# Row maxima of 384 and 512 keys taken by one fused VectorE instruction that adds the causal mask

## The chip, the cores and the metric

The kernel runs on one core of a Trainium2 chip. The metric is the device time of one execution in microseconds. The kernel before has a median of 1715.19 us over 3 runs (1712.28 to 1717.48).

## What is computed

The reference chains four layers over an input of 4 batches of 1024 tokens with 128 channels: a time-mixing layer with an exponential scan, a mixture of 16 small experts with grouped routing, a linear attention with decaying state ("deltanet"), and a causal softmax attention with grouped keys, followed by a mixture of 8 experts. The change concerns the causal softmax attention alone:

```python
def _gqa(x, wq, wk, wv, wo):
    q = (x @ wq.T).reshape(B, S, N_HEADS, HEAD_DIM)      # 16 heads of 8
    k = (x @ wk.T).reshape(B, S, N_KV_HEADS, HEAD_DIM)   # 4 key heads
    v = (x @ wv.T).reshape(B, S, N_KV_HEADS, HEAD_DIM)
    k = jnp.repeat(k, n_rep, axis=2)
    v = jnp.repeat(v, n_rep, axis=2)
    attn = jnp.einsum('bqhd,bkhd->bhqk', q, k) * scale
    causal = jnp.tril(jnp.ones((S, S), dtype=bool))
    attn = jnp.where(causal, attn, jnp.float32(-jnp.inf))
    attn = jax.nn.softmax(attn, axis=-1)
    out = jnp.einsum('bhqk,bkhd->bqhd', attn, v).reshape(B, S, C)
    return out @ wo.T
```

Here S is 1024 and B is 4. A softmax needs the largest score of each row. The kernel computes these row maxima in a pass of its own, ahead of the exponentials.

## The kernel before

Up to about 711 us of the span the first three layers run, in an order that a planner chooses from the program. From there on the order is written out by hand (`tc.manual_schedule()`): the causal attention of the four batches is worked in 32 blocks, one for each batch b and each i of 0 to 7, a block being 128 query rows of all 16 heads. Between the units of a block the same loop feeds in, one step per tick, the remaining linear attention of later batches and the building of queries and keys (`front`), and the last expert layer of earlier rows (`behind_it`). [...]

For block (b, i) the row maxima are computed by `maxima(b, i)`, two blocks before the block's weights (`AHEAD = 2`), and its units are interleaved with the units of `weighted`. A unit of `weighted` multiplies keys by queries (L945), takes the exponential on ScalarE (L950), masks the diagonal on GpSimd (L954), and later adds the product with the values (L937).

`maxima` splits the keys of a row into the half that holds the diagonal (`late`) and, for i of 4 and more, a full first half of 512 keys (`early`). The number of keys in the diagonal half is n_s = 128, 256, 384 or 512, by i % 4. [...] `late` puts 4, 2, 1 or 1 heads into one bank (`in_bank`). It issues one score matmul for each head (L874), then one matmul that adds the causal mask to the last 128 keys of each head in the bank (L878: the identity times `later`, a bf16 tile that holds 0 or -1e30), and then one maximum over the bank on VectorE (L882). `early` has no mask: a matmul (L886) and a maximum (L887). All of them share three PSUM banks (`to_max`, the tile name `sm`): a fourth matmul group waits until VectorE has read the first bank.

When the 16 heads are done, `rows` combines the two halves (L894), splits each maximum into three bf16 parts (L895 to L898), and, some ticks later, transposes them (L901), copies them out of PSUM (L905) and stores them by DMA into rows of the query tile (L909). The score matmul at L945 then subtracts the maximum as part of its product.

For i % 4 of 2 or 3 (384 or 512 keys) there is one head in a bank, so a block has 16 units of one score matmul, one mask matmul and one maximum. There are 16 such blocks in the four batches, so 256 such units. These are what the change touches. Other VectorE work that stands in the same queue: the state scans of the linear attention (L620), its products with the queries (L637), and the small operations of the last expert layer.

Of the kernel before, what the change touches and what calls it, by code (L numbers as in the profile page):

```python
# [12 lines left out]
BF = mybir.dt.bfloat16  # L13
AF = mybir.ActivationFunctionType
ALU = mybir.AluOpType
# [3 lines left out]
P = 128  # L19
NB = 4  # L20
T = 1024
CH = 512
# [12 lines left out]
def r3(ap, a):  # L35
    return ap.rearrange("p (a b) -> p a b", a=a)
# [3 lines left out]
def sandwich(ctx: ExitStack, tc: tile.TileContext, x, vecs, cmats, rope, wa, wb, wc, wd, out):  # L40
# [3 lines left out]
    nc = tc.nc  # L44
# [121 lines left out]
    def restarts(nb, n_e, pool, name):  # L166

        t = pool.tile([P, nb, n_e], FP, name=name, bufs=1)
        nc.gpsimd.memset(t, 1.0)
        nc.gpsimd.memset(t[:, :, 0:1], 0.0)  # L170
        return t
# [580 lines left out]
    pk = ctx.enter_context(tc.tile_pool(name="pk", bufs=1, side="left", reuse_waits="tile"))  # L752
# [8 lines left out]
    m = pe.tile([P, P], FP, tag="a", name="m", bufs=1)  # L761
    make_causal_mask(nc, m, MASKED)
    for k in range(4):
        nc.gpsimd.tensor_copy(later[:, k, :], m)
    wv_d, wo_d, wgate_d = wdt[:, 160:192], wdt[:, 192:320], wdt[:, 320:328]
    restart8 = restarts(4, 8, pk, "restart8")
    QSCALE = float(1.0 / np.sqrt(8).astype(np.float32))
# [22 lines left out]
    def later_on(ticks, fn):  # L790
        due.append((now[0] + ticks, fn))
# [67 lines left out]
    def maxima(b, i):  # L859


        qr, kr = qrs[b, i // 4], keys_r[b % 2]
        tb = slice(i % 4 * P, (i % 4 + 1) * P)
        half = i // 4
        n_s = (i % 4 + 1) * P
        in_bank = CH // n_s
        ms = pe.tile([P, 2, 16], FP, tag="ms", name="ms", bufs=3)

        def late(h0):
            sc = to_max([P, CH], "sm")  # L870
            view = r3(sc[:, : in_bank * n_s], in_bank)
            for k in range(in_bank):
                h = h0 + k
                nc.tensor.matmul(  # L874
                    view[:, k, :], lhsT=qr[0:KROWS, h, tb], rhs=kr[0:KROWS, half, h // 4, 0:n_s],
                    start=(k == 0), stop=False, skip_group_check=True,
                )
            nc.tensor.matmul(  # L878
                view[:, :, n_s - P :], lhsT=identb, rhs=later[:, :in_bank, :], start=False, stop=True,
                skip_group_check=True,  # L880
            )
            nc.vector.tensor_reduce(ms[:, 0, h0 : h0 + in_bank], view, AX.X, ALU.max)  # L882

        def early(h):
            sc = to_max([P, CH], "sm")
            nc.tensor.matmul(sc, lhsT=qr[0:KROWS, h, tb], rhs=kr[0:KROWS, 0, h // 4, :], start=True, stop=True)  # L886
            nc.vector.tensor_reduce(ms[:, 1, h : h + 1], sc, AX.X, ALU.max)  # L887

        def rows():
            mp = pe.tile([P, 3, 16], BF, tag="mp", name="mp", bufs=3)  # L890
            left = pe.tile([P, 16], FP, tag="ml", name="ml", bufs=3)
            top = ms[:, 0]
            if half:
                nc.vector.tensor_max(top, top, ms[:, 1])  # L894
            nc.vector.tensor_copy(mp[:, 0], top)  # L895
            nc.vector.tensor_sub(left, top, mp[:, 0])
            nc.vector.tensor_copy(mp[:, 1], left)
            nc.vector.tensor_sub(mp[:, 2], left, mp[:, 1])  # L898
            def turned():
                pm = to_max([48, P], "m_ps", BF)  # L900
                nc.tensor.transpose(pm, mp.rearrange("p i h -> p (i h)"), identb)  # L901

                def kept():
                    mt = pe.tile([48, P], BF, tag="mt", name="mt", bufs=3)
                    nc.vector.tensor_copy(mt, pm)  # L905

                    def placed():
                        for k in range(3):
                            nc.sync.dma_start(  # L909
                                out=qr[KROWS + k : KROWS + k + 1, :, tb], in_=mt[16 * k : 16 * k + 16, :]  # L910
                            )
                        placed_rows.add((b, i))

                    later_on(3, placed)

                later_on(1, kept)

            later_on(9, turned)

        units = [lambda h0=h0: late(h0) for h0 in range(0, 16, in_bank)]  # L920
        if half:
            units += [lambda h=h: early(h) for h in range(16)]
        return units + [rows]
# [243 lines left out]
    pd = ctx.enter_context(tc.tile_pool(name="pd", bufs=2, side="right", reuse_waits="tile"))  # L1167
# [111 lines left out]
```

## Time and profile before

| | |
|---|---|
| median of 3 runs | 1715.19 us |
| profiled execution | 1715.55 us |
| its span | 1713.8 us |
| TensorE busy | 1310.6 us, 76% |
| VectorE busy | 1168.9 us, 68% |
| ScalarE busy | 856.7 us, 50% |
| GpSimd busy | 655.9 us, 38% |
| DMA | 90.49 MB, mean 53 GB/s |
| mean granted TensorE clock | 0.85 |
| from 711 us to the end: TensorE, VectorE busy | 803.6 us, 672.3 us of 1002.8 |

The page gives, for one profiled execution on the chip, the busy time of each engine, the span in 40 slices, the chain of work that ended last, and the costliest groups of instructions. A group's row names the source line, the engine, the operation, output and input tiles with their shapes and the count; then its busy time and the mean duration of one; then the idle time of the engine just before it and what ended that idle time. PE is TensorE's matmuls, PEld its weight loads, DVE is VectorE, ACT ScalarE, POOL GpSimd, SP SyncE. [...] the busy time of a group can be more than the time the queue loses to it: two instructions of one engine can overlap in part. A wait names the waiting instruction and the one that released it, with the total, the count and the longest.

### The profile page before, as it was taken

Reading aid. Unit: us, or ns where it says so; the run is one execution under the profiler, and the core shown is the slowest. Engines: PE = TensorE matmul, PEld = TensorE weight load, DVE = VectorE, ACT = ScalarE, POOL = GpSimd, SP = SyncE. Lnnn points to the kernel's source line nnn. Section 1 sums busy time; section 2 is a strip of 40 time slices with the busy share of each in tenths; the row PEclk is TensorE's granted clock in tenths of the full one; section 3 lists DMA queues with packets and bytes.
Section 4 is the critical chain, followed back from the end, with each engine's and each line's share of the span. In section 5 each row is a group of like instructions: output and inputs, shape, how many; then the busy total and the mean of one; then the engine's idle time right before and its main releaser. Section 6 shows DMA issues by size and latency. Waiting matters only on the chain.

```text
span 1713.8 us, 15167 instructions
## 1 busy us (share of the span) xinstructions
PE 1310.6 (76%) x4593; PEld 463.3 (27%) x4604; DVE 1168.9 (68%) x1991; ACT 856.7 (50%) x1565; POOL 655.9 (38%) x663
## 2 busy tenths in 40 slices
PE   2547887867865889678779869888887879889864
PEld 1213333312221323133223223322232223233311
DVE  4575676698775877867995597777779825577601
ACT  3457776624453457234436625645553345645561
POOL 5554353524252324323433363427227333122212
PEclk8669998978887999877779869987898669989996
DMA  2000110313033122101112111231113011110101
GB/s 97 13 7 6 25 50 25 96 40 108 13 111 110 53 65 85 44 12 34 45 58 70 53 57 54 70 92 46 38 37 101 21 48 64 45 61 29 54 22 56
DMA packets 59330, 90.49 MB, mean 53 GB/s; under 512 B 9904, under 2 KB 26800, under 8 KB 58544
## 3 DMA queue, kind: packets, MB, share of 16 engines
q1 hardware_dynamic: 59248, 89.52, 17.3%
q8 instruction: 36, 0.59, 0.1%
q14 instruction: 46, 0.38, 0.1%
HBM read 76.38 MB, written 12.71 MB: 52 GB/s over the span
## 4 chain that ended last, share of the span: by engine, by line
PE 32%; DVE 18%; ACT 6%; issue 4%; POOL 4%; DMA 2%; SPq 0%; POOLq 0%; DVEq 0%; ACTq 0%
PE av L937 8%; PE sc L945 5%; DVE ms L882 4%; DVE st L620 4%; ACT pr L950 3%; PE sm L874 3%; DVE ms L887 3%; PE y L1074 3%; PE sm L886 2%; PE ln_v L138 2%; PE num_ps L674 1%; POOL hid L473 1%; POOL share L1062 1%; PE sm L878 1%; PE g_ps L138 1%
## 5 line engine op out<-in xcount | busy, mean ns | idle before, releaser
L950 ACT ACTIVATE pr<-sc 128x512 f32<-128x512 f32 x576 | 328.2, 595 | 361.7 <-PE sc L945 358.0
L882 DVE TENSOR_REDUCE ms<-sm 128x1 f32<-128x512 f32 (+3 forms) x352 | 210.5, 633 | 114.2 <-PE sm L878 103.0
L945 PE MATMUL sc<-qr,keys_r 75*128 75x512 bf16 x576 | 234.1, 422 | 37.7 <-ACT pr L950 28.7
L887 DVE TENSOR_REDUCE ms<-sm 128x1 f32<-128x512 f32 x256 | 165.0, 682 | 56.4 <-PE sm L886 55.9
L937 PE MATMUL av<-pr,va 128*32 128x512 f32 x1152 | 183.1, 710 | 0.0
L954 POOL TENSOR_SCALAR_AFFINE_SELECT pr<-pr 128x512 f32<-128x512 f32 x128 | 89.4, 712 | 244.5 <-ACT pr L950 236.2
L874 PE MATMUL sm<-keys_r,qr 72*128 72x512 bf16 (+3 forms) x512 | 138.2, 337 | 46.3 <-DVE ms L882 43.9
L138 PE MATMUL ln_v<-rs,cm 128*128 128x512 f32 x176 | 113.0, 733 | 43.0 <-ACT rs L126 28.3
L473 POOL TENSOR_TENSOR hid<-hid,gate 128x512 f32<-128x512 f32 x64 | 81.9, 1280 | 162.9 <-DVE hid L468 124.6
L614 POOL TENSOR_TENSOR kv<-vrep,phi 128x512 f32<-128x512 f32 x64 | 85.6, 1342 | 115.0 <-issue 47.9
L1062 POOL TENSOR_TENSOR share<-n,every 128x512 f32<-128x512 f32 x64 | 87.2, 1373 | 91.1 <-DMA every<-row 70.5
L455 PE MATMUL y_ps<-hid,wbt 128*128 128x512 f32 x144 | 84.1, 669 | 46.3 <-DVE hid L474 44.4
L886 PE MATMUL sm<-keys_r,qr 72*128 72x512 bf16 x256 | 99.6, 417 | 25.0 <-DVE ms L887 20.6
L945 PEld LDWEIGHTS <-keys_r 75*128 75x128 bf16 x576 | 58.7, 106 | 153.2 <-issue 126.3
L878 PE MATMUL sm<-later,identb 128*128 128x128 bf16 (+2 forms) x341 | 90.5, 265 | 0.0
L474 DVE TENSOR_TENSOR hid<-hid,g 128x512 f32<-128x512 f32 x72 | 57.7, 801 | 46.7 <-POOL hid L473 39.9
L138 PE MATMUL u_ps<-n,wbt 128*128 128x512 f32 x144 | 77.3, 618 | 7.6 <-DVE hid L468 5.1
L138 PE MATMUL g_ps<-n,wbt 128*128 128x512 f32 x144 | 78.8, 630 | 3.7 <-DVE hid L463 1.6
L1074 PE MATMUL y<-share,wexp 128*128 128x512 f32 x128 | 70.8, 644 | 9.6 <-POOL share L1062 9.4
L874 PEld LDWEIGHTS <-qr 72*128 72x128 bf16 x512 | 51.0, 107 | 99.4 <-issue 82.8
L465 ACT ACTIVATE g<-hid 128x512 f32<-128x512 f32 x72 | 45.1, 626 | 55.4 <-DVE hid L463 55.3
L674 PE MATMUL num_ps<-st,cm 128*32 128x512 f32 x128 | 52.5, 777 | 25.7 <-DVE st L637 25.5
(300 smaller groups left out, 2394.9 us busy)
## 6 DMA issues: line engine op xcount, KB each, us to landing
gate<-rows SPq DMA_DIRECT2D x64, 256.0 KB
vrep<-v_rows SPq DMA_DIRECT2D x64, 256.0 KB
every<-row SPq DMA_DIRECT2D x64, 256.0 KB
qr<-dq SPq DMA_DIRECT2D x72, 128.0 KB
turn<-in_rope_dram SPq DMA_DIRECT2D x8, 512.0 KB
dq<-qp SPq DMA_DIRECT2D x8, 384.0 KB
keys_r<-dk SPq DMA_DIRECT2D x72, 32.0 KB
sums<-av_sb SPq DMA_DIRECT2D x128, 18.0 KB
```

What stands on the lines that cost most here:

```text
L138: nc.tensor.matmul(ps, lhsT=lhsT, rhs=rhs, start=True, stop=True)
L473: nc.gpsimd.tensor_mul(a, a, gate)
L874: nc.tensor.matmul(view[:, k, :], lhsT=qr[0:KROWS, h, tb], rhs=kr[0:KROWS, half, h // 4, 0:n_s], start=(k == 0), stop=False, skip_group_ch ...
L878: nc.tensor.matmul(view[:, :, n_s - P :], lhsT=identb, rhs=later[:, :in_bank, :], start=False, stop=True, skip_group_check=True,)
L882: nc.vector.tensor_reduce(ms[:, 0, h0 : h0 + in_bank], view, AX.X, ALU.max)
L886: nc.tensor.matmul(sc, lhsT=qr[0:KROWS, h, tb], rhs=kr[0:KROWS, 0, h // 4, :], start=True, stop=True)
L887: nc.vector.tensor_reduce(ms[:, 1, h : h + 1], sc, AX.X, ALU.max)
L937: nc.tensor.matmul(pavs[b, i][32 * g : 32 * g + 32, :], lhsT=va[:, j, g, :], rhs=pr, start=(j == 0), stop=(j == i),)
L945: nc.tensor.matmul(sc, lhsT=kr[0:ROWS, j // 4, g, j % 4 * P : (j % 4 + 1) * P], rhs=qr[0:ROWS, 4 * g : 4 * g + 4, tb], start=True, stop=True,)
L950: nc.scalar.activation(pr, sc, AF.Exp)
L1062: nc.gpsimd.tensor_mul(shares[-1], n4, gates[len(shares) - 1])
L1074: nc.tensor.matmul(y, lhsT=wexp[:, e, :], rhs=shares[e], start=False, stop=(e == 7))
```

## The change

For 384 and 512 keys the mask matmul is left out, and the plain maximum is replaced by one instruction that adds a mask from SBUF and takes the maximum of the sum:

```diff
+    at_last = pk.tile([P, CH], BF, name="at_last")
+    nc.gpsimd.memset(at_last, 0.0)
+    nc.gpsimd.tensor_copy(at_last[:, CH - P :], m)
...
                 nc.tensor.matmul(
                     view[:, k, :], lhsT=qr[0:KROWS, h, tb], rhs=kr[0:KROWS, half, h // 4, 0:n_s],
-                    start=(k == 0), stop=False, skip_group_check=True,
+                    start=(k == 0), stop=(in_bank == 1), skip_group_check=True,
                 )
+            if in_bank == 1:
+
+                masked = pd.tile([P, CH], BF, tag="masked", name="masked", bufs=1)
+                nc.vector.tensor_tensor_reduce(
+                    masked[:, :n_s], sc[:, :n_s], at_last[:, CH - n_s :], 1.0, -3.0e38, ALU.add, ALU.max,
+                    ms[:, 0, h0 : h0 + 1],
+                )
+                return
             nc.tensor.matmul(
                 view[:, :, n_s - P :], lhsT=identb, rhs=later[:, :in_bank, :], start=False, stop=True,
                 skip_group_check=True,
```

`at_last` is a constant of 512 columns per partition in bf16: zero in the first 384, the causal mask in the last 128. The slice `at_last[:, CH - n_s :]` has the mask in its last 128 columns for either size. The instruction reads the scores from PSUM and the mask from SBUF, writes the masked scores as bf16 to `masked`, a buffer that nothing reads, and writes the maximum to `ms`. Blocks with 128 and 256 keys, and the unmasked first halves, keep their code. In the changed kernel the lines stand further down: the score matmul is L877, the fused instruction L884, the remaining mask matmul L889, the remaining plain maximum L893, the maximum of the first half L898.

## The prediction

> **What bounds the kernel now.** I read the chain of waits on the page first, then the groups by shape, the waits, and the timeline and stage sums where the changed line runs.
>
> ```profile
> PE 32%; DVE 18%; ACT 6%; issue 4%; POOL 4%; DMA 2%; SPq 0%; POOLq 0%; DVEq 0%; ACTq 0%
> PE av L937 8%; PE sc L945 5%; DVE ms L882 4%; DVE st L620 4%; ACT pr L950 3%; PE sm L874 3%; DVE ms L887 3%; PE y L1074 3%; PE sm L886 2%; PE ln_v L138 2%; PE num_ps L674 1%; POOL hid L473 1%; POOL share L1062 1%; PE sm L878 1%; PE g_ps L138 1%
> ```
>
> No engine sets the end alone: TensorE leads, VectorE is second, and the row maxima (L882, 4%) stand among the dearest links. The mask matmul (L878) is 1%.
>
> ```profile
> L882 DVE TENSOR_REDUCE ms<-sm 128x1 f32<-128x512 f32 x128 | 82.3, 683 | 28.3 <-PE sm L878 28.3
> L882 DVE TENSOR_REDUCE ms<-sm 128x1 f32<-128x384 f32 x128 | 64.7, 546 | 21.2 <-PE sm L878 21.0
> L878 PE MATMUL sm<-later,identb 128*128 128x128 bf16 x256 | 62.5, 244 | 0.0
> L468 DVE TENSOR_TENSOR hid<-u_ps,hid 128x512 f32<-128x512 f32 x72 | 49.1, 682 | 15.0 <-PE u_ps L138 10.1 <-ACT g L465 3.9 <-ACT ho L699 0.7
> L620 DVE TENSOR_TENSOR_SCAN st<-beta_ps,kv 128x512 f32<-128x512 f32 x32 | 38.0, 1209 | 7.6 <-POOL kv L614 7.6
> ```
>
> The first three rows are exactly what changes: 256 maxima and their 256 mask matmuls. The last two are the nearest rows to the new instruction.
>
> ```profile
> DVE ms L882 <- PE sm L878: 103.0, 73, 7.1
> PE sm L874 <- DVE ms L882: 43.9, 44, 4.4
> ```
>
> Both engines wait on each other around the three PSUM buffers of `to_max`: VectorE for the last matmul of a bank, TensorE for a bank to be read. The 103 us are not the price of the mask matmul. With it gone, VectorE waits for the score matmul just before it.
>
> The 256 units come in 16 stretches of 16 (blocks with i % 4 of 2 or 3, four batches). Each stretch runs from the first to the last of its reductions; four of the 16, and their sum:
>
> ```profile
> 1008.35:1026.93 18.58, 14.15 (x68) 5.08 (x69) 18.53 (x26) 6.17 (x11) 10.88 (x9) 0.68 0.12 34
> ...
> 1392.24:1418.98 26.74, 23.10 (x92) 8.61 (x91) 14.78 (x41) 15.30 (x29) 10.49 (x11) 0.74 0.26 81
> 1484.31:1492.77 8.46, 7.45 (x48) 3.52 (x47) 7.83 (x17) 3.35 (x6) 2.54 (x4) 1.00 0.27 79
> 1493.53:1505.79 12.26, 9.76 (x49) 3.30 (x48) 10.01 (x18) 5.43 (x10) 3.29 (x5) 0.86 0.34 97
> ...
> sum 266.73, PE 219.68 PEld 84.29 DVE 209.38 ACT 116.41 POOL 86.89; mean PE 13.73 PEld 5.27 DVE 13.09 ACT 7.28 POOL 5.43
> ```
>
> Columns: length, then busy time of PE, PEld, DVE, ACT, POOL, then the granted clock. Length less DVE busy is VectorE's slack. In time order, over all 16: 2.0, 3.6, 1.4, 3.6, 1.1, 0.0, 5.2, 8.5, 2.6, 3.3, 1.8, 12.0, 0.6, 2.3, 6.1, 3.4; together 57 us. These stretches are where the change is decided.
>
> **Removed: 256 mask matmuls and their weight loads.** The group says 244 ns each, 62.5 us, but that is latency. Spacing is what the queue pays:
>
> ```profile
> 887.57 0.22 PE L878 MATMUL sm<-later,identb 128*128 128x128 bf16 x1
> 887.57 0.10 PEld L945 LDWEIGHTS <-keys_r 75*128 75x128 bf16 x1
> 887.63 0.38 PE L945 MATMUL sc<-qr,keys_r 75*128 75x512 bf16 x1
> ```
>
> The next matmul starts 0.06 us after the mask matmul; at a lower clock, at 889.65, 0.11 us. [...] So 62 us by the mean, [...] 15 to 28 us by the two spacings; I take the trace's 0.06 to 0.11, 1.0 to 1.8 us per stretch. It helps only where TensorE, not VectorE, sets the pace, at most in the stretches with large slack.
>
> **Added: the fused instruction.** Streaming 512 numbers from PSUM with a second operand from SBUF and a full write to SBUF costs 682 ns in L468, and the plain maximum costs 683. By these two rows fusion is free. [...] VectorE's queue grows by 256, each fused instruction followed by a 128x1 one. And 232 of the 256 wait for VectorE itself as well as for TensorE, since `masked` is a single buffer. No run here shows their durations, so I build the unit from this stretch:
>
> ```profile
> 1484.31 3.44 DVE L882 TENSOR_REDUCE ms<-sm 128x1 f32<-128x384 f32 x7
> 1487.67 0.20 DVE L905 COPY mt<-m_ps 48x128 bf16<-48x128 bf16 x1
> 1487.80 2.40 DVE L882 TENSOR_REDUCE ms<-sm 128x1 f32<-128x384 f32 x5
> 1490.82 1.95 DVE L882 TENSOR_REDUCE ms<-sm 128x1 f32<-128x384 f32 x4 [0.62 <-PE sm L878]
> 1492.81 0.18 DVE L895 CAST mp<-ms 128x16 bf16<-128x16 f32 x1
> 1493.02 0.17 DVE L896 TENSOR_TENSOR ml<-ms,mp 128x16 f32<-128x16 f32 x1
> ```
>
> Five reductions of 546 ns take 2.40, so one starts every 0.464 us: an independent instruction starts 0.08 before its predecessor ends. A dependent one (the cast at 1492.81, ended 1492.99, then 1493.02) starts 0.03 after. Small ops last 0.17. A 512-key unit now takes 0.68 - 0.08 = 0.60. Fused: 0.60 to the start of the accumulator read, 0.17 for it, 0.03 until the next may start: 0.80. The same for 384 keys (0.47 to 0.67). So +0.20 us per unit, 51 us over 256, 3.2 us per stretch.
>
> Bounds: if the accumulator read has to wait for the main instruction's end, 0.68 + 0.03 + 0.17 + 0.03 = 0.91, +0.31. If the read lasts only 0.06 (the start spacing of the small maxima at 1520.22, four in 0.37), +0.09. A body that runs like the scan (1209) would add far more (+0.7), but a running maximum was already carried at 683 by the reduction, so I leave this in the tail. I take 0.20, because the small VectorE ops are the nearest rows to a 128x1 one and the read carries no wait.
>
> **How much shows.** If slack absorbed all it could, only 3.2 less slack would remain per stretch: 1.2 + 1.8 + 2.1 + 3.2 + 0.6 + 1.4 + 2.6 + 0.9 = 13.8 us. But slack is partly hand-over latency between the two engines, and a longer reduction frees its bank later. With half the slack usable the remainder is 26.4. Midway: 20 us. Behind a waiting fused instruction stand, in VectorE's queue, the front's scans (L620) and products (L637), for which TensorE's L674 waits, the splits at L895 to L898 and the copies `mt`. They move by the same 3 us; the row of maxima is prepared two blocks ahead, so its DMAs do not become late. TensorE's queue, blocked on a bank, delays L945 and so the exponentials.
>
> TensorE's return: in the four stretches with slack over 5 us it still leads, 4 x (1.0 to 1.8), about 5 us. Net +15.
>
> **The rest.** On GpSimd, one memset of 128x512 and one cast of 128x128 (0.28 like L764) near 320 us; the memset is under 1 us by the 128x1024 one (two in 1.83). The queue is full there until 335, then waits 3.25 us for VectorE, which hides it; uncovered, 1 us. The planner also moves a few matmuls and POOL memsets against each other between 320 and 460 us, with the same instructions: 0, plus or minus 3. From 711 us on the order is hand-written and the built program differs only in the replaced units. SyncE's queue is unchanged, so no transfer moves except with its producer.
>
> Sum: 1715.55 (profiled execution, span 1713.8) + 20 - 5 = **1730.5 us**; the median of the runs is 0.4 lower, inside their spread.
>
> **Rivals.** (1) Faster: TensorE's share decides. If the accumulator read costs +0.09, VectorE adds 1.4 us per stretch, of which about 4 us in all show, while 12 stretches return 1.0 to 1.8, about 15: 1704. For it: TensorE is 82% busy in the stretches, VectorE 78%. Against: the small ops' 0.17. The turning point is near +0.12 per unit. (2) A draw, within 5 us: exposed and returned time cancel. (3) Much slower: the read waits for the main instruction[...]: +0.31, and with half the slack usable 52 us: 1768; with none, 79: 1795. For it: the self-wait and the second instruction make every hand-over serial. That the mask matmuls stay is excluded by the program (512 fewer TensorE instructions).
>
> **Chances.** Forecast 0.55 (1720 to 1750), rival 1 0.17, draw 0.11, rival 3 0.17. A change below 0.3% (5 us, about what the runs' spread can tell) counts as the same. Range 1706 to 1770: below it half of rival 1, above it half of rival 3.
>
> **What would show it.** In the profile after: two VectorE groups at the fused line, about 0.68/0.55 and 0.17 us; start spacing 0.80 and 0.67; slack in the stretches near zero and TensorE's wait for VectorE grown from 43.9; L878 down to 96 instructions. I am wrong if the spacing stays at 0.6, or if the stretches lengthen by much more or less than 20 us, or if time moves ahead of 711 us.

## The result and the profile after

The changed kernel takes 1732.70 us (median of 10 runs, 1728.84 to 1742.70), the kernel before, run beside it, 1721.29 us (10 runs, 1712.28 to 1730.57). The ratio is 1.0081, with a 95% interval of 1.0061 to 1.0100: slower by some 14 us. The forecast was +15, from 1715.55 to 1730.5 us. Executions more than 1.5% above the fastest of the same kernel are left out of the ratios here and below, and one profile, the second of the kernel of experiment 2, is of such an execution.

The profiled execution of after took 1742.70 us, the longest of its ten, so its span of 1741.0 us is not to be set against the 1713.8 us of before. The chain of waits of after:

```profile
PE 31%; DVE 19%; issue 7%; ACT 6%; POOL 4%; DMA 1%; SPq 0%; POOLq 0%; DVEq 0%; ACTq 0%
PE av L948 7%; PE sc L956 5%; DVE masked L884 4%; DVE ms L898 3%; PE y L1085 3%; PE sm L877 3%; ACT pr L961 3%; DVE st L620 3%; PE ln_v L138 2%; PE sm L897 2%; POOL hid L473 1%; PE num_ps L674 1%; DVE ms L893 1%; PE g_ps L138 1%; DVE hid L474 1%
```

The fused instruction (L884) stands at 4%. L882 had 4% before, but with the 96 maxima of the short rows in it (128 and 256 keys), and those are now L893 with another 1%. VectorE's part of the chain grew, from 18% to 19%.

The changed groups of after, by shape, and VectorE's timeline in a dense stretch:

```profile
L884 DVE CUSTOM_DVE_ANT_0 masked<-sm,at_last 128x512 bf16<-128x512 f32 x128 | 88.1, 688 | 32.7 <-PE sm L877 23.0 <-DVE ms L884 0.5
L884 DVE CUSTOM_DVE_ANT_0 masked<-sm,at_last 128x384 bf16<-128x384 f32 x128 | 70.7, 552 | 23.5 <-PE sm L877 11.9 <-DVE ms L884 1.0
L884 DVE DVE_READ_ACCUMULATOR2_ANT ms<- 128x1 f32 x256 | 21.1, 82 | 0.0
```

```profile
1497.01 0.56 DVE L884 CUSTOM_DVE_ANT_0 masked<-sm,at_last 128x384 bf16<-128x384 f32 x1
1497.49 0.08 DVE L884 DVE_READ_ACCUMULATOR2_ANT ms<- 128x1 f32 x1
1497.72 0.56 DVE L884 CUSTOM_DVE_ANT_0 masked<-sm,at_last 128x384 bf16<-128x384 f32 x1
...
1511.18 0.69 DVE L884 CUSTOM_DVE_ANT_0 masked<-sm,at_last 128x512 bf16<-128x512 f32 x1
1511.80 0.08 DVE L884 DVE_READ_ACCUMULATOR2_ANT ms<- 128x1 f32 x1
1512.02 0.69 DVE L884 CUSTOM_DVE_ANT_0 masked<-sm,at_last 128x512 bf16<-128x512 f32 x1
```

The main instruction streams as fast as the plain maximum (688 and 552 ns against 683 and 546). The second instruction, a read of the accumulator, starts 0.07 to 0.08 us before the first ends and lasts 0.08. Then VectorE stands still for about 0.15 us (1497.57 to 1497.72): the next main instruction waits for this accumulator read (`<-DVE ms L884` in the rows above; in experiment 4, without that wait, a unit of 384 keys starts every 0.51 us). So a unit starts every 0.71 us (384 keys) or 0.84 us (512), where it was 0.47 and 0.60. For 512 keys this is read from a row of before, eight reductions in 4.92 us:

```profile
1499.26 4.92 DVE L882 TENSOR_REDUCE ms<-sm 128x1 f32<-128x512 f32 x8 [1.92 <-PE sm L878]
```

The same four of the 16 stretches in after, and the sum over all 16 (length, busy time of PE, PEld, DVE, ACT, POOL, granted clock, DMA):

```profile
1023.60:1044.17 20.57, 15.74 (x55) 3.99 (x56) 18.66 (x42) 6.51 (x11) 10.95 (x9) 0.58 0.10 30
...
1405.43:1432.58 27.15, 21.17 (x83) 7.25 (x82) 15.57 (x57) 15.92 (x30) 10.97 (x12) 0.81 0.28 80
...
1497.01:1509.59 12.58, 9.89 (x31) 2.67 (x30) 9.18 (x34) 3.40 (x6) 2.56 (x5) 0.61 0.31 88
1510.35:1526.19 15.84, 13.82 (x43) 3.56 (x43) 11.30 (x34) 6.14 (x11) 3.80 (x5) 0.50 0.22 63
...
sum 285.58, PE 227.73 PEld 70.44 DVE 223.43 ACT 120.50 POOL 88.89; mean PE 14.23 PEld 4.40 DVE 13.96 ACT 7.53 POOL 5.56
```

The 16 stretches together grew from 266.7 to 285.6 us, the dense pair at 1484 and 1493 us by 4.1 and 3.6. Two things stand out. TensorE executes a quarter fewer instructions in the dense pair (31 and 43 for 48 and 49), yet is busy longer, and its granted clock there fell from 1.00 and 0.86 to 0.61 and 0.50. And slack did not vanish: 285.6 less 223.4 is 62 us, after 57 before. About 20 us of it is now VectorE's wait for itself, which counts as idle: in the timeline of after, 136 fused instructions start 0.15 us after the accumulator read just before them.

### The profile page after: what moved, and what is told of

Read it like the earlier page. It is cut to its first block, busy times and chain, and to the rows that moved or that the text cites. A ratio compares the mean times of both kernels' runs of the same rounds, so it can differ in the third digit from the quotient of the medians.

```text
span 1741.0 us, 15146 instructions
## 1 busy us (share of the span) xinstructions
PE 1333.2 (77%) x4337; PEld 453.2 (26%) x4348; DVE 1177.7 (68%) x2247; ACT 858.0 (49%) x1565; POOL 655.4 (38%) x665
## 4 chain that ended last, share of the span: by engine, by line
PE 31%; DVE 19%; issue 7%; ACT 6%; POOL 4%; DMA 1%; SPq 0%; POOLq 0%; DVEq 0%; ACTq 0%
PE av L948 7%; PE sc L956 5%; DVE masked L884 4%; DVE ms L898 3%; PE y L1085 3%; PE sm L877 3%; ACT pr L961 3%; DVE st L620 3%; PE ln_v L138 2%; PE sm L897 2%; POOL hid L473 1%; PE num_ps L674 1%; DVE ms L893 1%; PE g_ps L138 1%; DVE hid L474 1%
## 5 line engine op out<-in xcount | busy, mean ns | idle before, releaser
L956 PE MATMUL sc<-qr,keys_r 75*128 75x512 bf16 x576 | 242.1, 435 | 37.4 <-ACT pr L961 29.7
L898 DVE TENSOR_REDUCE ms<-sm 128x1 f32<-128x512 f32 x256 | 165.7, 682 | 66.0 <-PE sm L897 65.7
L884 DVE CUSTOM_DVE_ANT_0 masked<-sm,at_last 128x384 bf16<-128x384 f32 (+1 forms) x256 | 158.8, 620 | 56.2 <-PE sm L877 34.9
L948 PE MATMUL av<-pr,va 128*32 128x512 f32 x1152 | 187.2, 722 | 0.0
L877 PE MATMUL sm<-keys_r,qr 72*128 72x512 bf16 (+3 forms) x512 | 144.8, 360 | 51.7 <-DVE ms L884 42.9
L138 PE MATMUL ln_v<-rs,cm 128*128 128x512 f32 x176 | 113.1, 734 | 45.9 <-ACT rs L126 30.8
L897 PE MATMUL sm<-keys_r,qr 72*128 72x512 bf16 x256 | 104.0, 437 | 21.6 <-DVE ms L898 17.3
L893 DVE TENSOR_REDUCE ms<-sm 128x2 f32<-128x512 f32 (+1 forms) x96 | 63.6, 682 | 58.9 <-PE sm L889 48.6
L138 PE MATMUL u_ps<-n,wbt 128*128 128x512 f32 x144 | 80.8, 644 | 6.1 <-DVE hid L468 4.8
L877 PEld LDWEIGHTS <-qr 72*128 72x128 bf16 x512 | 51.1, 111 | 130.8 <-issue 116.5
L138 PE MATMUL g_ps<-n,wbt 128*128 128x512 f32 x144 | 80.4, 641 | 3.3 <-DVE hid L463 1.7
```

Of the source, the lines that this page charges most:

```text
L138: nc.tensor.matmul(ps, lhsT=lhsT, rhs=rhs, start=True, stop=True)
L877: nc.tensor.matmul(view[:, k, :], lhsT=qr[0:KROWS, h, tb], rhs=kr[0:KROWS, half, h // 4, 0:n_s], start=(k == 0), stop=(in_bank == 1), skip ...
L884: nc.vector.tensor_tensor_reduce(masked[:, :n_s], sc[:, :n_s], at_last[:, CH - n_s :], 1.0, -3.0e38, ALU.add, ALU.max, ms[:, 0, h0 : h0 + 1],)
L948: nc.tensor.matmul(pavs[b, i][32 * g : 32 * g + 32, :], lhsT=va[:, j, g, :], rhs=pr, start=(j == 0), stop=(j == i),)
L956: nc.tensor.matmul(sc, lhsT=kr[0:ROWS, j // 4, g, j % 4 * P : (j % 4 + 1) * P], rhs=qr[0:ROWS, 4 * g : 4 * g + 4, tb], start=True, stop=True,)
```

## The experiments

Theory A was the prediction's: the unit is longer on VectorE, and that is the loss. Two rivals came from the profile of after. **B**: the first stretch began 13 us later, so the loss lies in the planned part of the program ahead of 711 us. **C**: fewer matmuls lower the granted clock (0.85 to 0.827 over the span), and that is the loss. In all experiments I use two readings: the time of all runs beside the kernel before, and the summed length of the 16 stretches in the profile, with the clock in them.

**1. The constant alone.** The kernel before, with `at_last` built and not used.

```diff
+    at_last = pk.tile([P, CH], BF, name="at_last")
+    nc.gpsimd.memset(at_last, 0.0)
+    nc.gpsimd.tensor_copy(at_last[:, CH - P :], m)
```

> The kernel before, with the mask constant of 512 columns built on GpSimd but used by nothing. Theory A (the fused unit is longer on VectorE by about 0.24 us, and that is the loss): within 3 us of before. Rival B (the other order that the planner chooses before 711 us is the loss; in the profile the first stretch already starts 13 us later): +10 to +14 us. Rival C (fewer matmuls lower the granted TensorE clock, which was 0.85 in the profile before and 0.827 after): within 3 us, clock as before.

Measured: 1718.18 us against 1719.83 for the kernel before, ratio 1.0000 (0.9967 to 1.0033); stretches 266.8 us at clock 0.79. B's +10 to +14 is out. The planner's order is that of after here too, so the order costs less than the interval allows, 6 us.

**2. TensorE's part alone.** The kernel before without the 256 mask matmuls.

```diff
-                    start=(k == 0), stop=False, skip_group_check=True,
+                    start=(k == 0), stop=(in_bank == 1), skip_group_check=True,
                 )
-            nc.tensor.matmul(
+            if in_bank > 1:
+              nc.tensor.matmul(
```

> The kernel before, without the 256 mask matmuls for 384 and 512 keys, and with the plain maximum; no constant. The maximum is then taken over masked keys too: a larger number is subtracted from the scores, which the softmax allows. This is TensorE's part of the change alone. Theory A: -5 us (between -2 and -15), the maxima start every 0.60 and 0.47 us as before. Rival B: 0, or a gain, but nothing of the +14. Rival C: slower than before or equal, with a clock near 0.83.

Measured: 1715.72 us, ratio 1.0000 (0.9967 to 1.0033). A's -5 us do not show; the expectation that is met is C's (equal, at a lower clock: 0.841 over the span). The stretches did not shrink. The dense pair and the sum:

```profile
1480.55:1490.54 9.99, 8.98 (x30) 2.62 (x29) 7.90 (x18) 3.20 (x6) 2.56 (x5) 0.65 0.29 91
1491.29:1505.54 14.25, 13.91 (x50) 3.73 (x49) 10.30 (x18) 6.64 (x12) 3.80 (x5) 0.56 0.26 77
...
sum 269.35, PE 222.82 PEld 67.78 DVE 210.45 ACT 117.13 POOL 87.62; mean PE 13.93 PEld 4.24 DVE 13.15 ACT 7.32 POOL 5.48
```

With VectorE's work untouched, both dense stretches are 1.5 to 2 us longer than in the profile of before, at a clock of 0.65 and 0.56 for 1.00 and 0.86. That pair alone proves little: the second profile of before (experiment 5) has a 384-key stretch just as long. The mean clock of all 16 stretches is 0.725 against 0.79, and the score matmul of 512 keys lasts longer. In before, and here:

```profile
L874 PE MATMUL sm<-keys_r,qr 72*128 72x512 bf16 x128 | 54.4, 443 | 14.8 <-DVE ms L882 14.5
L874 PE MATMUL sm<-keys_r,qr 72*128 72x512 bf16 x128 | 59.7, 507 | 13.2 <-DVE ms L883 12.3
```

That the slower clock took back what the missing matmuls freed is the likely reading. If the mask matmuls had been off the path in the first place, the stretches would be as long too; this run does not tell the two apart.

**3. VectorE's part alone.** The kernel after with the mask matmul put back ahead of the fused instruction.

```diff
-                    start=(k == 0), stop=(in_bank == 1), skip_group_check=True,
+                    start=(k == 0), stop=False, skip_group_check=True,
                 )
+            nc.tensor.matmul(
+                view[:, :, n_s - P :], lhsT=identb, rhs=later[:, :in_bank, :], start=False, stop=True,
+                skip_group_check=True,
+            )
             if in_bank == 1:
```

> The kernel after with the mask matmul put back in front of the fused instruction, so the mask is added twice. This is VectorE's part alone. Theory A: slower than after by what the mask matmul costs, +20 to +26 us over before. Rival B: as after, +12 to +14. Rival C: as before, since all matmuls are back, with a clock as before.

Measured: 1745.83 us, ratio 1.0148 (1.0099 to 1.0196), +25 us; stretches 296.3 us, clock in them 0.704.

```profile
sum 296.34, PE 249.46 PEld 92.16 DVE 222.55 ACT 118.92 POOL 88.90; mean PE 15.59 PEld 5.76 DVE 13.91 ACT 7.43 POOL 5.56
```

As A said, and C in its simple form is out: with every matmul back, the clock is low all the same. Why is not shown. TensorE's wait for the maxima is no longer than before, 41.8 us against 43.9. And beside the fused instruction the mask matmuls do cost time: after, which lacks them, is 8 to 11 us faster than this kernel (1.0081 and, repeated in experiment 5, 1.0101), and its stretches are 11 to 14 us shorter (285.6 and 282.7).

**4. Without the wait for itself.** The masked scores are written back into the PSUM bank, so that no shared buffer makes a fused instruction wait for the one before.

```diff
-                masked = pd.tile([P, CH], BF, tag="masked", name="masked", bufs=1)
...
-                    masked[:, :n_s], sc[:, :n_s], at_last[:, CH - n_s :], 1.0, -3.0e38, ALU.add, ALU.max,
+                    sc[:, :n_s], sc[:, :n_s], at_last[:, CH - n_s :], 1.0, -3.0e38, ALU.add, ALU.max,
```

> The kernel after, but the fused instruction writes its masked scores back into the PSUM bank it reads, so that there is no shared buffer and nearly no wait of VectorE for itself (7 of 256 left, before 232). The accumulator read stays. Theory A with the self-wait as its main term: the start spacing falls from 0.85 and 0.71 us to about 0.65 and 0.52, and the time to between -8 and +3 us of before. If the accumulator read is the main term, the spacing stays over 0.75 and the time at +10 or more. Rivals B and C: the time stays at +12 to +14 whatever the spacing.

> The fused instruction that writes back into its PSUM bank, once more. If removing VectorE's wait for itself returns about 9 us in the stretches: 273 to 278 us for them again, at a start spacing of 0.52 and 0.65. If the first profile was chance: 280 to 286, as after. The time: 1.004 to 1.008 of before.

Measured: ratios 1.0075 (1.0046 to 1.0105) and 1.0118 (1.0041 to 1.0195); stretches 275.5 and 277.7 us. VectorE's timeline in the second profile:

```profile
1495.99 0.14 DVE L883 DVE_READ_ACCUMULATOR2_ANT ms<- 128x1 f32 x1
1495.99 0.60 DVE L883 CUSTOM_DVE_ANT_0 sm<-sm,at_last 128x384 f32<-128x384 f32 x1
1496.50 0.14 DVE L883 DVE_READ_ACCUMULATOR2_ANT ms<- 128x1 f32 x1
1496.50 0.60 DVE L883 CUSTOM_DVE_ANT_0 sm<-sm,at_last 128x384 f32<-128x384 f32 x1
```

The accumulator read and the next main instruction start together, every 0.51 us. So of the 0.24 us by which the unit grew, the wait for itself is 0.20, and the second instruction 0.05. (The edit also moves the masked scores from SBUF in bf16 to PSUM in fp32; a second buffer in SBUF was not tried.) The stretches are about 8 us shorter than after's, as A said. The time did not follow: both ratios lie above the range that A gave for this spacing, and at after's. The intervals are too wide to say whether those 8 us show in the time at all. So the wait for itself is shown to be most of what the unit grew by; that it is most of the lost time is not shown.

**5. Second profiles of before, of after, and of the kernel without the 256 mask matmuls.** Nothing is edited.

> The kernel before once more, for a second profile. Theory A (the loss is made in the 16 stretches of the 256 maxima, and the rest of the difference between the profiles of before and after is where the granted clock happens to change in each execution): the stretches last 267 us together again, within 3, at a clock near 0.79, while the start of the first stretch may lie anywhere from 758 to 772 us. Rival B (the time ahead of 711 us belongs to the kernel): the first stretch starts at 759 us again, within 2.

> The kernel after once more. Theory A: the stretches last 286 us again, within 4, at a clock near 0.72; the first stretch may start anywhere from 758 to 772 us; the time is +11 to +17 us over before. Rival B: the first stretch starts at 772 us again, within 2.

> The kernel before without the 256 mask matmuls, with the plain maximum over masked keys too, once more. If TensorE's share returns nothing because its clock falls in the stretches: 269 us for the stretches again, within 3, at a clock near 0.725 against 0.79, and a time within 5 us of before. If the first run of it was chance: stretches near 260 us, and 5 us or more faster than before.

Measured: before 1708.08 us (one run), stretches 271.4 us at 0.77, longer than A's 267 within 3, first stretch at 761.5 us. Its dense pair:

```profile
1475.28:1485.45 10.17, 9.47 (x45) 3.98 (x44) 7.91 (x17) 2.99 (x6) 2.55 (x4) 0.67 0.30 84
1486.21:1499.04 12.83, 12.50 (x65) 4.57 (x63) 10.13 (x18) 6.58 (x12) 3.30 (x5) 0.76 0.28 80
```

The same program, in an execution that is 7.5 us shorter as a whole, takes 10.17 us for the 384-key stretch at 0.67, where it took 8.46 at 1.00. So without any edit such a stretch can come out 1.7 us longer at a lower clock, and the length of one stretch does not tell the time of the kernel.

After 1735.08 us, ratio 1.0101 (1.0051 to 1.0151), stretches 282.7 us at 0.715, first stretch at 764.7 us. Without the mask 1715.71 us, ratio 0.9960 (0.9928 to 0.9992). That is 7 us faster than before, where the first series had no difference and 5 us at most were expected. Its stretches, 276.3 us at 0.716, are longer than expected, but in an execution of 1724.64 us, well over its median; that length is not used below. The stretches of after repeat within 3 us; the start of the first moves by 7.5. The last transpose of the input (L233), ahead of which all these programs are alike, starts at 238 to 246 us in different executions. Ahead of that, the 14 matmuls of `ln_c` (L138) last 646 ns on the mean in the first profile of before and 760 in the first of after.

One part of the start does belong to the change. From the last GpSimd addition at L345 to the first at L483 takes 20.9 to 21.4 us in all eight profiles without the constant, and 23.6 to 23.7 us in all six with it: the two instructions that build the constant (0.8 us) and the planner's other order cost 2.5 us there. It is not made up again: from that addition to the first stretch it is 440.2 to 441.3 us without the constant and 443.1 to 444.3 with it. In the second profile of after:

```profile
320.88 1.26 POOL L345 TENSOR_TENSOR xT<-xT,r 128x512 f32<-128x512 f32 x1
...
322.93 0.52 POOL L766 MEMSET at_last<- 128x512 bf16 x1
...
344.50 1.64 POOL L483 TENSOR_TENSOR xT<-xT,rs 128x512 f32<-128x512 f32 x1 [1.74 <-DVE rs L482]
```

**6. No mask matmul at all.** The maxima are taken over masked keys for every size.

```diff
-                    start=(k == 0), stop=False, skip_group_check=True,
+                    start=(k == 0), stop=(k == in_bank - 1), skip_group_check=True,
                 )
-            nc.tensor.matmul(
-                view[:, :, n_s - P :], lhsT=identb, rhs=later[:, :in_bank, :], start=False, stop=True,
-                skip_group_check=True,
-            )
```

> The kernel before without any of the 352 mask matmuls in the row maxima; the maxima are taken over masked keys too, for every size. The 96 further matmuls are wider (256 and 512 columns). If the clock eats what TensorE gives back: within 5 us of before, as without the 256. If the wider ones stand on the path: 5 to 12 us faster than before.

Measured: ratio 1.0024 (0.9999 to 1.0049), stretches 268.8 us at 0.72. Leaving out 352 matmuls brings nothing that can be measured.

**7. More matmuls instead of fewer.** If the clock gives back what a matmul takes, doubling the mask matmul should cost nothing.

```diff
+            if in_bank == 1:
+                nc.tensor.matmul(
+                    view[:, :, n_s - P :], lhsT=identb, rhs=later[:, :in_bank, :], start=False, stop=False,
+                    skip_group_check=True,
+                )
             nc.tensor.matmul(
                 view[:, :, n_s - P :], lhsT=identb, rhs=later[:, :in_bank, :], start=False, stop=True,
```

> The kernel before with the mask matmul of the 256 units issued twice. If a mask matmul costs its queue time (0.06 to 0.11 us) on the path: the stretches grow by 5 to 25 us from 268. If the granted clock makes up for it: the stretches stay within 4 us of 268, the clock in them rises over 0.79, and the time stays within 5 us of before.

Measured: 1707.49 us against 1716.59, ratio 0.9961 (0.9935 to 0.9987): faster than before in this series, by a little more than the 5 us expected at most.

```profile
1481.09:1489.74 8.65, 8.11 (x65) 4.48 (x64) 7.85 (x17) 3.29 (x6) 2.55 (x4) 1.00 0.28 85
1490.50:1503.38 12.88, 11.39 (x73) 4.83 (x74) 10.04 (x18) 6.11 (x12) 3.35 (x5) 0.87 0.35 102
...
sum 265.81, PE 222.41 PEld 96.88 DVE 210.72 ACT 118.25 POOL 87.48; mean PE 13.90 PEld 6.05 DVE 13.17 ACT 7.39 POOL 5.47
```

TensorE executes 65 instructions in the first of these stretches where it had 48, and the stretch is 0.2 us longer than before. The mean clock in all stretches is 0.84, and their sum 265.8 us, no longer than in before's profiles (266.7 and 271.4). With none, one and two mask matmuls in a unit the clock in the stretches is 0.72, 0.79 and 0.84. Two more kernels ask how far this goes: one with a further matmul, overwritten at once, ahead of each `early` score matmul, and one with four mask matmuls.

```diff
+            nc.tensor.matmul(sc[:, 0:P], lhsT=identb, rhs=later[:, 0, :], start=True, stop=True)
             nc.tensor.matmul(sc, lhsT=qr[0:KROWS, h, tb], rhs=kr[0:KROWS, 0, h // 4, :], start=True, stop=True)
```

```diff
+            for _ in range(3 if in_bank == 1 else 0):
+                nc.tensor.matmul(
```

> Two mask matmuls for each of the 256 units, and in front of each of the 256 score matmuls of the first halves one more 128-column matmul whose result is overwritten. If the granted clock goes on paying for the added work: clock over 0.86 and 0 to 8 us faster than with two masks alone (0.992 to 0.996 of before). If the added queue time (256 times 0.06 to 0.11) now stands on the path: 0.998 to 1.008 of before.

> Four mask matmuls for each of the 256 units. If the clock in the stretches, 0.72, 0.79 and 0.84 with none, one and two, has little left to rise: clock in the stretches near 0.9, but 512 more matmuls of at least 0.06 us, so the stretches grow over 270 us and the time is 0.998 to 1.01 of before. If clock still pays: below 266 us and 0.993 or less.

Measured: 1.0016 (0.9994 to 1.0039) with the filler in `early`, overall clock 0.864; 0.9964 (0.9939 to 0.9989) with four masks, stretches 269.3 us, clock in them 0.875. Four lie in neither of the two ranges expected of them. Two are as good as four, and in `early` added work is a draw at best. Why two gain 7 us where the stretches gain 1 to 6 is not settled: the rest of that profile is shorter too, but so is the rest in the second profile of before.

## Why the prediction was right, and where it was not

The time and the sign were right, +14 us for a forecast of +15, and the place was right: the stretches. The longer unit on VectorE is the cause: the constant alone loses nothing (experiment 1), fewer matmuls alone lose nothing (2), each within 6 us, and the fused instruction loses time with the mask matmuls in place (3). The terms were not all right.

- **The unit on VectorE: the right cause, the size nearly.** Predicted +0.20 us, measured +0.24. Its make-up was wrong. I gave the accumulator read 0.17 us and the step to the next instruction 0.03, after the small VectorE rows; it takes 0.08 and then 0.15. One difference stands in the trace: a separate wait instruction goes with 232 of the 256 (21 ns each); the rows that I took (L895, L896) have none. Whether it makes the 0.15 is not shown: no run has the wait for itself without that instruction. Experiment 4 shows the wait for itself to be 0.20 of the 0.24.
- **How much of it shows.** Predicted 20 of 51 us. The stretches without the 256 mask matmuls are 269.4 us, those of after 285.6 and 282.7, mean 284.1. That is about 15 of 62 us, less than half, as assumed; the usable half of the slack was an estimate of mine. With the mask matmuls in both kernels it is more: 25 us of time (17 to 34, experiment 3). That the slack would go to zero was wrong: it is 62 us, some 20 of them the wait for itself, which is counted as idle time. TensorE's wait for the maxima grew as I said, but only from 43.9 to 48.9 us. The hand-overs that I took for a part of the slack are short where I can read one of each in before: 0.04 us from the end of a mask matmul (1490.56, 0.22 long) to the maximum at 1490.82, and 0.05 us from the end of that maximum (0.56 long) to the score matmul that waited for it, at 1491.43.
- **TensorE's return: the step that failed.** I let the freed queue time return 5 us in the stretches where TensorE leads. These runs show no such fixed price. Beside the plain maximum the return is 0 in one series and 7 us in the other (experiments 2 and 5), the stretches do not shrink, and the granted clock in them falls from 0.77 or 0.79 to 0.72; experiment 7 shows the reverse. Beside the fused instruction it is 8 to 11 us (experiment 3 against after). The matmul was priced by its spacing at a given clock (0.06 us near 888 us, where the granted clock was 1.00, and 0.11 near 890 us, where it was 0.50), as if neither the clock nor the price could change. The first profile already had the column that would have warned: 0.68 to 1.00 in the four stretches shown there.
- **The constant and the planner: 0, plus or minus 3.** Measured +2.5 us, at the place named.
- **Sum.** The runs give 10.5 to 17.2 us (the interval of the ratio on 1721.29 us). Taken apart with the mask matmuls removed first, the profiles give 15 - 0 + 2.5; removed last, the runs give 25 less 8 to 11. The forecast's 20 - 5 lies between the two. In the first order a missing return and the planner were covered by a VectorE term some 5 us high; in the second both terms were too small. That their sum fell about 1 us from the measured 14 is in part luck.
- **The rivals.** The faster one needed an accumulator read below +0.12 per unit and TensorE's return. Experiment 4 gives the first, +0.05, and is still slower than before: the return of 15 us that the rival counted on is not there. The draw is out, since the ratio's interval begins at 1.0061. The much slower one is out, since the read does not wait for the main instruction's end (it starts 0.07 to 0.08 us ahead of it); but its argument that the wait for itself makes the units serial came true, at +0.24 between my +0.20 and its +0.31.

## What to carry to other kernels

The fused VectorE instruction here is two instructions, and with one throw-away output buffer for all units, 232 of the 256 wait for the one before: 0.20 of the 0.24 us by which the unit grew (experiment 4). Look for that wait in the built program before counting what fusion saves. And here, where TensorE alternates with VectorE, 256 small matmuls taken out returned 0 us in one series and 7 in the other: read the granted clock of the stretch along with its busy time, and compare several profiles, since one stretch of one kernel came out at 1.00 and at 0.67. When two things change at once, undo each alone: the same 256 matmuls were worth 0 to 7 us beside the plain maximum and 8 to 11 beside the fused instruction.

## What was not expected of the hardware

Beside the plain maximum, the granted clock in the stretches rises with single small matmuls: 0.72 with no mask matmul in a unit (experiments 2 and 6), 0.77 to 0.79 with one (three profiles), 0.84 with two, 0.875 with four. In the stretch of 384 keys near 1484 us alone it is 0.65 and 0.68 with none and 1.00 with two or four; with one it is 1.00 twice and 0.67 once. Beside the fused instruction it does not rise: 0.704 with the mask matmul, 0.72 and 0.715 without. What decides the granted clock is not shown by these runs. That added, useless matmuls could make the kernel 0.4% faster (0.9961 with two, 0.9964 with four) was not expected by either reading. It is not secure: the ratio of one and the same kernel moved as much between two series (1.0000 and 0.9960, without the mask), and with filler in `early` as well it is 1.0016.

The fused instruction with a PSUM output and no wait has its accumulator read and the next main instruction start at the same instant. The read then takes 0.14 us for 0.08 and the main one 0.60 for 0.56; whether the overlap or the output in PSUM does this is not shown.
